# The order of the turned maxima, the sums and one normalised source in a transformer block

## The chip, the cores and the metric

The kernel runs on one core of a Trainium2 chip. The metric is the device time of one execution in microseconds (us), here the median of three runs. Beside it one further execution was profiled; all instruction times below come from that one.

## The reference

The block works on 16 sequences of 256 tokens with 256 features, all in float32, with 16 heads of 16 features:

```python
x_norm = modulate(_ln(x), shift_a, scale_a)
q, k, v = split(x_norm @ W_qkv + b_qkv)
x = x + gate_a * (softmax(q @ k.T / 4) @ v @ W_proj + b_proj)      # self-attention
q_c = _ln(x) @ W_qc + b_qc
k_c, v_c = split(_ln(context) @ W_kvc + b_kvc)
x = x + softmax(q_c @ k_c.T / 4) @ v_c @ W_cproj + b_cproj         # cross-attention
h = gelu(modulate(_ln(x), shift_m, scale_m) @ W_mlp1 + b_mlp1) @ W_mlp2 + b_mlp2
x = x + gate_m * h
```

shift, scale and gate come from `silu(cond) @ W_mod + b_mod`, one row per sequence. `_ln` subtracts a token's mean and divides by its standard deviation.

## The kernel before, in words

**Units and beats.** The 32 attentions (16 self, kind "s", and 16 cross, kind "c") are units, numbered 0 to 31: s0 to s4 first, then s and c in turn (unit 5 is s5, unit 6 is c0, and so on to unit 26, which is c10), then c11 to c15 as units 27 to 31. So an even unit between 6 and 26 is a cross-attention, an odd one from 5 to 25 a self-attention. After the units comes the MLP, which the change does not touch. A unit takes eight beats; `beat(n, k)` writes down all the work of beat k of unit n, for several units at once: unit n (`cur`) is being exponentiated and summed, unit n-1 (`prev`) is finishing, for unit n+1 (`nxt`) the row maxima are found, and the units n+2 to n+4 (`q2`, `q3`, `q4`) are being normalised, transposed and projected; `p1`, `p2`, `p3` are the output parts of the units n-1 to n-3. `lc`, `ls` and `lx` say of which kind such a unit is: `lx` is unit n+3 if that is a cross-attention (its source, the self-attention's result, is then normalised in this unit), `lc` is unit n+4 if cross, `ls` if self.

**Every engine runs its instructions in the order of the code.** A wrapper (`InOrder`, line 51, which is why the profile puts nearly all instructions on L51) keeps the program's order on TensorE, VectorE, ScalarE, GpSimd and the DMA queue of SyncE. So an instruction that waits holds up everything behind it on its engine.

**What a beat holds.** `visit` comes first: four matmuls into `s` (scores of unit n+1, from which VectorE takes row maxima into `mx`, a TENSOR_REDUCE), then four into `st` (scores of unit n in the other orientation). Then ScalarE turns `st` into exponentials `pt`. `s` and `st` have one buffer each: the next beat's `s` waits for this beat's reduce, its `st` for this beat's exponentials. In even beats `av_part` follows: 16 matmuls into `o` (values and, in a column of ones, sums). In odd beats a stretch of twelve pairs of projections (`lanes`) follows. In beats 0 and 2 two of the four transposes each of unit n+3's normalised source into `psT` (`turn`) stand behind `o`; where unit n+3 is a cross-attention, the four transposes of its other source (`psT_q`) stand behind `o` of beat 4.

**The maxima.** They must be subtracted before the exponential. That is done inside the matmul: row 63 of a half of `q` holds minus the maximum, row 63 of `k` holds ones. `m_part` does it twice per unit: it transposes `mx` (128x16) on TensorE into `psm`, negates it on ScalarE into `m`, and SyncE's DMA queue writes `m` into `q`. The second half of a unit's maxima is turned in its beat 0 (needed in its beat 4), the first half one beat 4 earlier, under the name `nxt` (needed in its beat 0).

**Banks.** `psm`, `psT` and `o` share two PSUM banks (tag "tr"); a tile gets the bank that came free first, and its first writer waits until the last reader of the tile before in that bank is done. `ps_k`, `ps_q`, `ps_v` and `ps_P` share two others in the same way (tag "gen"): in beat 5 `ps_k` gets the bank of `ps_q`, which VectorE reads last when it makes `l_q` (cross: `l_qc`) in beat 4.

**Sums and values.** When `o` of beat 2 or of beat 6 is copied to `oT` on ScalarE (`o_out`), `pull` fetches the sums `S` and the values `U` out of it by DMA; VectorE takes the reciprocal of `S` in beat 2 (in beat 3 where unit n+4 is a self-attention), `spread` and `back` bring it over DRAM into `R`, and GpSimd multiplies `U` by it in the next unit's beat 0 (`norm`, `high`, `low`), for the projection `ps_P` in beat 3.

**The last normalised source.** In beat 1, `lx.ln[1].steps` gets the statistics of unit n+3's self-attention result and normalises its two token tiles on GpSimd (`xn_q`, two TENSOR_SCALARs). For unit 31, that is in unit 28's time, the statistics are only taken in that beat.

Of the kernel before, what the change touches and what calls it, by code (L numbers as in the profile page):

```python
# [16 lines left out]
P = 128  # L17
# [4 lines left out]
def pixart_block(  # L22
# [273 lines left out]
    def layernorm(src, name):  # L296

        o = Box()

        def stats():  # L300
            o.st = work.tile([P, NT, 6], F32, tag="bnst", bufs=4, name=f"st_{name}")
            for t in range(NT):
                DVE.bn_stats(o.st[:, t], src()[:, t])

        def rstd(power=True):
            o.mv = work.tile([P, NT, 2], F32, tag="bnmv", bufs=4, name=f"mv_{name}")
            for t in range(NT):
                DVE.bn_aggr(o.mv[:, t], o.st[:, t])
            o.rs = work.tile([P, NT], F32, tag="rstd", bufs=4, name=f"rs_{name}")
            if power:  # L310
                o.pow()

        def pow():
            POOL.tensor_scalar(o.rs, o.mv[:, :, 1], EPS, None, ALU.add)
            POOL.tensor_tensor(o.rs, o.rs, mhalf, ALU.pow)

        def apply(eng=E_['LN'].get(name[0])):
            o.xn = work.tile([P, NT, H], F32, tag="xn", name=f"xn_{name}", bufs=3)
            if eng == "act":
                nb = work.tile([P, NT], F32, tag="rstd", name=f"nb_{name}", bufs=4)  # L320
                DVE.scalar_tensor_tensor(nb, o.mv[:, :, 0], -1.0, o.rs, ALU.mult, ALU.mult)
            for t in range(NT):
                if eng == "act":
                    ACT.activation(o.xn[:, t], src()[:, t], AF.Identity, bias=nb[:, t:t + 1],
                                   scale=o.rs[:, t:t + 1])
                else:
                    (DVE if eng == "dve" else POOL).tensor_scalar(
                        o.xn[:, t], src()[:, t], o.mv[:, t, 0:1], o.rs[:, t:t + 1],
                        ALU.subtract, ALU.mult)

        def stat(t):
            if t == 0:
                o.st = work.tile([P, NT, 6], F32, tag="bnst", bufs=4, name=f"st_{name}")
            DVE.bn_stats(o.st[:, t], src()[:, t])

        o.steps, o.pow, o.stat = [stats, rstd, apply], pow, stat
        return o
# [216 lines left out]
    def build_post(u):  # L554
# [15 lines left out]
            o.xg = work.tile([P, NT, H], F32, tag="xg", name=f"xg_{b}")  # L570
            POOL.tensor_tensor(o.xg, X[b], bc_t(G[b][:, 1]), ALU.add)

        def pull(G):

            if G == 0:
                o.U = work.tile([P, KC, N], F32, tag="U", name=f"U_{name}")
                o.S = work.tile([P, 32], F32, tag="S", name=f"S_{name}")
            SP.dma_start(o.S[64 * G:64 * G + 64], u.oT[1:98:32, G])
            SP.dma_start(o.U[64 * G:64 * G + 64], u.oT[0:P - 1:2, G])

        def recip():
            DVE.reciprocal(o.S, o.S)
# [82 lines left out]
                              AX.X, ALU.max)  # L665
        yield

    def m_part(u, hf):

        pst = ps_gen(f"psm_{u.n}_{hf}", SHORT)  # L670
        PE.transpose(pst[:16, :P], u.mx[:, hf].rearrange("p r a t -> p (r a t)"), ident)
        m = work.tile([16, P], F32R, tag="m", name=f"m_{u.n}_{hf}", bufs=1)
        ACT.mul(m, pst[:16, :P], -1.0)
        SP.dma_start(u.q[63:P:64, 4 * hf:4 * hf + 4, :].bitcast(F32), m.bitcast(F32))
# [19 lines left out]
    def exps():  # L694

        for f in later:
            f()
        later.clear()
# [275 lines left out]
        in_turn(*t)  # L974
        later.append(lambda: exp(units[n], k))

    def spare(n):
        p1, _, p3 = (v and v.post for v in map(unit, (n - 1, n - 2, n - 3)))
        if p3 and not p3.added:
            p3.add()  # L980
        if p1:
            p1.gate()

    def beat(n, k):
# [24 lines left out]
                p2.end()  # L1009
        visit(n, k)  # L1010
        if k == 0:
            if cur:
                m_part(cur, 1)
            exps()
            if q3 and q3.ready:
                q3.T[0].place()
            if prev:
                av_part(prev, 3)
            if q3 and q3.ready:
                q3.T[0].turn((0,))  # L1020
            if q2:
                q2.K.low()
                q2.K.send_low()
            if p2:
                p2.norm()
# [2 lines left out]
        elif k == 1:  # L1028
            exps()
            run(lanes(q2 and q2.Q, q2 and n and q2.V))  # L1030
            if prev:
                p1.pull(1)
            if lc:
                lc.ln[0].steps[0]()
            if lx:
                if lx.b in (0, B - 1):
                    lx.ln[1].steps[0]()
                lx.ln[1].steps[1]()
                lx.ln[1].steps[2]()
        elif k == 2:  # L1040
            exps()
            if cur:
# [10 lines left out]
        elif k == 3:  # L1053
# [14 lines left out]
            if prev and ls:  # L1068
                p1.recip()
                p1.spread()  # L1070
        elif k == 4:
            if nxt and lx:
                m_part(nxt, 0)
            exps()
            if nxt and not lx:
                m_part(nxt, 0)
            if alone:
                p2.end()
            if cur:
                av_part(cur, 1)  # L1080
            if lx:
                lx.T[1].turn()
            if q2:
# [1 line left out]
                q2.Q.send_low()  # L1085
            if q3 and q3.kind == "c":
                q3.T[0].rest_pool()
                spare(n)
            if ls:
                ls.ln[0].steps[1]()  # L1090
                ls.ln[0].steps[2]()
# [15 lines left out]
        elif k == 6:  # L1107
# [12 lines left out]
            if lx:  # L1120
                lx.T[1].full()
                lx.T[1].rest_pool()
        elif k == 7:
            exps()
            run(q3.vk if q3 and p2 else lanes(q3 and q3.V, q3 and q3.K))
# [110 lines left out]
```

## Time and profile before

| | |
|---|---|
| median of 3 runs | 748.76 us (744.28 to 749.36) |
| the profiled execution | 742.45 us, of which the program's span is 740.7 us |
| mean granted TensorE clock | 0.999 |
| busy in the span | TensorE 98%, its weight loads 81%, VectorE 77%, ScalarE 75%, GpSimd 71% |
| median instruction: transpose into psm | 277 ns, its weight load 87 ns, 64 of them |
| units 1 to 28 in the profile | about 15.8 us each where unit n+3 is a self-attention, 16.2 us where it is a cross-attention |

In the rows of the timeline stand: start in us from the span's start, duration in us, engine, line, operation, out<-in by the program's names, shapes, and how many instructions were merged into the row; in brackets the time for which the engine was idle before, and what ended it. PE is TensorE, PEld its weight loads, DVE VectorE, ACT ScalarE, POOL GpSimd, SPq the DMA queue of SyncE. The matmuls overlap, so what a matmul costs is read from the start of one to the start of the next, not from its duration.

### The profile page before, as it was taken

The numbers are of one execution on the slowest core, as the hardware profiler recorded it, in microseconds if no ns is written. First come the engines' busy times: TensorE is split into PE (matmuls) and PEld (weight loads), VectorE is DVE, ScalarE is ACT, GpSimd is POOL, SyncE is SP. The second block draws the span as 40 slices with busy tenths as digits, with TensorE's granted clock in tenths as the row PEclk, the third lists the DMA queues.
The fourth block names the chain that finished last, engine by engine and source line by source line (L and its number), as shares of the span: only waits on it lengthen the run. The fifth ranks groups of instructions, "written<-read, shape, count | busy, mean of one in ns | idle before, by whom it ended". The sixth has DMA issues, their size and how long they took to land.

```text
span 740.7 us, 22556 instructions
## 1 busy us (share of the span) xinstructions
PE 722.2 (98%) x9003; PEld 598.4 (81%) x9003; DVE 569.4 (77%) x882; ACT 556.1 (75%) x972; POOL 528.5 (71%) x525
## 2 busy tenths in 40 slices
PE   9999999999999999999999999999899999999997
PEld 8677777777777777777777787776479999999997
DVE  4778888878888887878788878778766877777762
ACT  5567888888888888887888888887766666666663
POOL 8465678797866868777686899985757676665663
PEclk9999999999999999999999999999999999999999
DMA  8365455544445455454555645545323132231311
GB/s 269 128 217 171 146 169 172 177 163 167 162 144 192 153 182 197 141 161 161 187 173 171 204 151 196 166 149 181 111 76 101 58 86 65 64 87 44 86 53 48
DMA packets 81388, 106.15 MB, mean 143 GB/s; under 512 B 16450, under 2 KB 44388, under 8 KB 81284
## 3 DMA queue, kind: packets, MB, share of 16 engines
q1 hardware_dynamic: 80180, 103.92, 43.3%
q8 instruction: 71, 1.16, 0.7%
q10 hardware_dynamic: 1104, 0.79, 0.4%
q14 instruction: 33, 0.27, 0.1%
HBM read 35.89 MB, written 8.98 MB: 61 GB/s over the span
## 4 chain that ended last, share of the span: by engine, by line
PE 92%; DVE 3%; ACT 2%; DMA 1%; issue 1%; POOL 1%; SPq 0%; ACTq 0%; POOLq 0%
PE s L51 18%; PE o L51 16%; PE st L51 14%; PE ph L51 13%; PE ps_P_s L51 4%; PE ps_k L51 3%; PE ps_v_s L51 3%; PE ps_kc L51 3%; PE ps_qc L51 3%; PE ps_v_c L51 2%; PE ps_q L51 2%; PE ps_P_c L51 2%; DVE mx L51 2%; PE psm L51 2%; PE psT_c L51 2%; PE psT_s L51 1%
## 5 line engine op out<-in xcount | busy, mean ns | idle before, releaser
L51 DVE TENSOR_REDUCE mx<-s 128x4 f32<-128x1024 f32 x252 | 307.7, 1221 | 89.2 <-PE s L51 88.7
L51 ACT ACTIVATE pt<-st 128x1024 f32<-128x1024 f32 x256 | 262.3, 1024 | 62.3 <-PE st L51 62.0
L51 PE MATMUL o<-pt,v 128*32 128x256 f32 x2048 | 137.1, 385 | 0.0
L51 PE MATMUL s<-big 63*128 63x256 f32 x1008 | 119.1, 307 | 5.5 <-DVE mx L51 4.0
L51 PE MATMUL st<-big 64*128 64x256 f32 (+1 forms) x1040 | 109.5, 284 | 3.1 <-ACT pt L51 1.7
L51 POOL TENSOR_TENSOR hl<-hf,hh 128x512 fp32r<-128x512 f32 x64 | 84.3, 1335 | 28.1 <-ACT hh L51 28.1
L51 PEld LDWEIGHTS s<-big 63*128 63x128 f32 x1008 | 79.0, 185 | 30.4 <-DVE mx L51 16.1
L51 PEld LDWEIGHTS st<-big 64*128 64x128 f32 (+1 forms) x1040 | 82.7, 186 | 6.6 <-ACT pt L51 3.4
L51 PEld LDWEIGHTS o<-pt,v 128*32 128x32 f32 x2048 | 53.4, 109 | 38.5
L51 ACT ACTIVATE hf<-ph,bT 128x256 f32<-128x256 f32 x120 | 50.4, 473 | 27.9 <-PE ph L51 27.9
L51 ACT ACTIVATE hh<-ph,bT 128x256 fp32r<-128x256 f32 x120 | 50.5, 472 | 20.9 <-PE st L51 9.8
L51 PE MATMUL ph<-wqch,wself 128*128 128x256 f32 x256 | 51.8, 286 | 1.3 <-ACT hh L51 1.3
L51 PE MATMUL ph<-wkch,wself 128*128 128x256 f32 x256 | 51.8, 286 | 0.0
L51 DVE TENSOR_SCALAR xn_m<-x,mv_m,rs_m 128x256 f32<-128x256 f32 x32 | 38.4, 1239 | 16.0 <-POOL rs_m L51 16.0
L51 PE MATMUL s<-big,hh 128*128 128x256 f32 x256 | 45.3, 276 | 0.0
L51 PE MATMUL st<-big,hh 128*128 128x256 f32 x256 | 45.0, 276 | 0.0
L51 PEld LDWEIGHTS ph<-wqch,wself 128*128 128x128 f32 x256 | 41.9, 191 | 1.9 <-ACT hh L51 1.5
L51 PEld LDWEIGHTS ph<-wkch,wself 128*128 128x128 f32 x256 | 41.9, 191 | 0.3
L51 POOL TENSOR_SCALAR xn_q<-x,mv_q,rs_q 128x256 f32<-128x256 f32 x32 | 38.9, 1225 | 1.7
L51 POOL TENSOR_SCALAR xn_c<-c,mv_c,rs_c 128x256 f32<-128x256 f32 x32 | 38.9, 1225 | 1.7
L51 PEld LDWEIGHTS s<-big,hh 128*128 128x128 f32 x256 | 38.8, 188 | 0.0
L51 PEld LDWEIGHTS st<-big,hh 128*128 128x128 f32 x256 | 38.8, 188 | 0.0
(214 smaller groups left out, 2215.7 us busy)
## 6 DMA issues: line engine op xcount, KB each, us to landing
big<-h_kc SPq DMA_DIRECT2D x32, 256.0 KB
big<-h_qc SPq DMA_DIRECT2D x32, 256.0 KB
big<-h_k SPq DMA_DIRECT2D x31, 256.0 KB
big<-h_q SPq DMA_DIRECT2D x31, 256.0 KB
big<-l_k SPq DMA_DIRECT2D x16, 256.0 KB
big<-l_q SPq DMA_DIRECT2D x16, 256.0 KB
g<-gd SPq DMA_DIRECT2D x16, 256.0 KB
U_s<-oT SPq DMA_DIRECT2D x32, 128.0 KB
```

Source lines behind the costliest of these rows:

```text
L51: i = f(*a, **k)
```

## The change

**Beat 0.** The transpose of the unit's second half of maxima moves from ahead of `o` to behind it, and no longer has a tile of its own: it writes into the upper half of the `psT` tile that the two transposes of unit n+3's source, right behind it, fill from below (in units 1 to 28; later there is no `psT`, and the maxima keep their own tile). ScalarE's negation moves from ahead of the exponentials to behind the copy `oT`. The pull of the sums moves from beat 1 to beat 0, ahead of the DMA of `l_k` (`send_low`); the pull of the values stays.

**Beat 4.** Where unit n+3 is a self-attention (units 0, 1, 2 and the even ones to 22), the transpose of the next unit's first half of maxima moves from ahead of `o` to behind it.

**Unit 28.** Only the first token tile of unit 31's source is normalised on GpSimd; the second is normalised on ScalarE in beat 4, between the negated maxima and the exponentials, with a bias that VectorE works out in beat 3. **Units 24 and 26.** The sum `xg` on GpSimd (`gate`) moves from beat 4 to beat 6.

```diff
+        def apply_half(t):
+            if t == 0:
+                o.xn = work.tile([P, NT, H], F32, tag="xn", name=f"xn_{name}", bufs=3)
+                POOL.tensor_scalar(o.xn[:, t], src()[:, t], o.mv[:, t, 0:1], o.rs[:, t:t + 1],
+                                   ALU.subtract, ALU.mult)
+            else:
+                ACT.activation(o.xn[:, t], src()[:, t], AF.Identity, bias=o.nb[:, t:t + 1],
+                               scale=o.rs[:, t:t + 1])
+        def apply_bias():
+            o.nb = work.tile([P, NT], F32, tag="rstd", name=f"nb_{name}", bufs=4)
+            DVE.scalar_tensor_tensor(o.nb, o.mv[:, :, 0], -1.0, o.rs, ALU.mult, ALU.mult)
...
-    def m_part(u, hf):
+    def m_part(u, hf, pst=None):
+        m_row(u, hf, m_turn(u, hf, pst))
-        pst = ps_gen(f"psm_{u.n}_{hf}", SHORT)
+    def m_turn(u, hf, pst=None):
+        if pst is None:
+            pst = ps_gen(f"psm_{u.n}_{hf}", SHORT)
         PE.transpose(pst[:16, :P], u.mx[:, hf].rearrange("p r a t -> p (r a t)"), ident)
+        return pst
+    def m_row(u, hf, pst):
         m = work.tile([16, P], F32R, tag="m", name=f"m_{u.n}_{hf}", bufs=1)
         ACT.mul(m, pst[:16, :P], -1.0)
         SP.dma_start(u.q[63:P:64, 4 * hf:4 * hf + 4, :].bitcast(F32), m.bitcast(F32))
...
         if k == 0:
-            if cur:
-                m_part(cur, 1)
             exps()
-            if q3 and q3.ready:
-                q3.T[0].place()
             if prev:
                 av_part(prev, 3)
             if q3 and q3.ready:
+                q3.T[0].place()
+                pst = m_turn(cur, 1, q3.T[0].ps[:, N:])
                 q3.T[0].turn((0,))
+            else:
+                pst = m_turn(cur, 1)
+            m_row(cur, 1, pst)
             if q2:
                 q2.K.low()
+            if prev:
+                p1.pull_sums(1)
+            if q2:
                 q2.K.send_low()
...
         elif k == 1:
...
             if prev:
-                p1.pull(1)
+                p1.pull_values(1)
...
-                lx.ln[1].steps[2]()
+                if lx.b == B - 1:
+                    lx.ln[1].apply_half(0)
+                else:
+                    lx.ln[1].steps[2]()
...
+            if lx and lx.b == B - 1:
+                lx.ln[1].apply_bias()
         elif k == 4:
             if nxt and lx:
                 m_part(nxt, 0)
+            if lx and lx.b == B - 1:
+                lx.ln[1].apply_half(1)
             exps()
-            if nxt and not lx:
-                m_part(nxt, 0)
             if alone:
                 p2.end()
             if cur:
                 av_part(cur, 1)
+            if nxt and not lx:
+                m_part(nxt, 0)
...
-                spare(n)
+                spare(n, not lc)
...
         elif k == 6:
...
                 lx.T[1].rest_pool()
+                if lc:
+                    p1.gate()
```

The added `apply_bias` call stands at the end of beat 3.

Beat 0 of unit 17 on TensorE and on the DMA queue. The rows name an operation, what it writes and reads, and a shape; `mx` are the maxima, `xn_c` the normalised source of unit 20, `o_2` the values of unit 16, `st` and `s` the scores. Before, the beat's first rows, up to the first matmuls into `o`, and then its last ones, from the last matmuls into `o` to the next beat's `s` and `st`:

```order
L51 MATMUL s<-big_75 128x256 x4
L51 MATMUL st<-big_77 128x256 x4
L51 MATMUL psm_1_5791<-ident,mx_5478 16x128
L51 MATMUL o_2_5722<-pt_6_5720,v_79 32x256
```

```order
L51 MATMUL o_2_5722<-pt_6_5720,v_79 32x256
L51 MATMUL o_2_5722<-pt_7_5747,v_79 32x256
L51 MATMUL psT_c_5798<-ident,xn_c_5704 128x128 x2
L51 MATMUL s<-big_75 128x256 x4
L51 MATMUL st<-big_77 128x256 x4
```

With the change, the end of the same beat:

```order
L51 MATMUL o_2_5706<-pt_6_5704,v_79 32x256
L51 MATMUL o_2_5706<-pt_7_5731,v_79 32x256
L51 MATMUL psT_c_5786<-ident,mx_5463 16x128
L51 MATMUL psT_c_5786<-ident,xn_c_5688 128x128 x2
L51 MATMUL s<-big_75 128x256 x4
L51 MATMUL st<-big_77 128x256 x4
```

The maxima's transpose has moved from between `st` and `o` to between `o` and `psT`, into the tile of `psT`. On the DMA queue the same beat and the next read, before and with the change (`m_1` the maxima, `l_kc` a part of unit 20's keys; here at unit 18):

```order
L51 DMA big_76<-h_kc_6726 32x4x512 x2
L51 DMA big_77<-m_1_6743 2x8x128
L51 DMA big_76<-l_kc_6760 32x4x512
L51 DMA S_s_6683<-oT_6649 64x1x32
L51 DMA U_s_6682<-oT_6649 64x512
```

```order
L51 DMA big_76<-h_kc_6707 32x4x512 x2
L51 DMA big_77<-m_1_6737 2x8x128
L51 DMA S_s_6664<-oT_6630 64x1x32
L51 DMA big_76<-l_kc_6740 32x4x512
L51 DMA U_s_6663<-oT_6630 64x512
```

The sums have passed one DMA. Beat 4 of unit 22 on TensorE, an even unit (`o_0` its own values, `mx` the maxima of unit 23, `ps_k` the keys of unit 25 in beat 5), before and then with the change from the last inputs of `o` on:

```order
L51 MATMUL st<-big_76 128x256 x4
L51 MATMUL psm_0_7527<-ident,mx_7362 16x128
L51 MATMUL o_0_7450<-pt_2_7448,v_79 32x256
L51 MATMUL o_0_7450<-pt_3_7482,v_79 32x256
```

```order
L51 MATMUL o_0_7428<-pt_2_7426,v_79 32x256
L51 MATMUL o_0_7428<-pt_3_7460,v_79 32x256
L51 MATMUL psm_0_7513<-ident,mx_7341 16x128
L51 MATMUL s<-big_77 128x256 x4
L51 MATMUL st<-big_76 128x256 x4
L51 MATMUL ps_k_7533<-xTh_s_7456,wself 128x256
```

The transpose now stands between `o` and the next beat's `s`. Beat 4 of unit 28 on ScalarE with the change (`h_qc` the queries of unit 30, `m_0` the maxima of unit 29, `x_15` the self-attention result of the last sequence, `pt_4` the exponentials); before, the fourth row was not there:

```order
L51 ACTIVATE pt_3_9396<-st 128x1024
L51 ACTIVATE h_qc_9425<-ps_qc_9319,bP 128x256 x2
L51 ACTIVATE m_0_9441<-psm_0_9439 16x128
L51 ACTIVATE xn_q_9354<-x_15_9263,nb_q_9423,rs_q_9351 128x256
L51 ACTIVATE pt_4_9445<-st 128x1024
L51 ACTIVATE pt_5_9474<-st 128x1024
```

Half of the normalisation has come in ahead of the exponentials.

More of the change, by code (lines that the diff above doesn't have):

```diff
@@ L578, in pull, with pull_values @@
             SP.dma_start(o.S[64 * G:64 * G + 64], u.oT[1:98:32, G])
+        def pull_values(G):
             SP.dma_start(o.U[64 * G:64 * G + 64], u.oT[0:P - 1:2, G])
+        def pull(G):
+            pull_sums(G)
+            pull_values(G)
+        o.pull_sums, o.pull_values = pull_sums, pull_values
         def recip():
@@ L975, in visit, with spare @@
         later.append(lambda: exp(units[n], k))
-    def spare(n):
+    def spare(n, gate=True):
         p1, _, p3 = (v and v.post for v in map(unit, (n - 1, n - 2, n - 3)))
@@ L980, in spare @@
             p3.add()
-        if p1:
+        if p1 and gate:
             p1.gate()
```

3 lines of the change are left out of this document (2 added, 1 removed).

## The prediction

> **What bounds the kernel now.** I read the page first: which engine is busy, and which carries the chain that ended last.
>
> ```profile
> PE 722.2 (98%) x9003; PEld 598.4 (81%) x9003; DVE 569.4 (77%) x882; ACT 556.1 (75%) x972; POOL 528.5 (71%) x525
> PE 92%; DVE 3%; ACT 2%; DMA 1%; issue 1%; POOL 1%; SPq 0%; ACTq 0%; POOLq 0%
> ```
>
> TensorE is busy for 98% of the span and makes 92% of the chain. Nothing that another engine saves counts by itself; what counts is TensorE's pace from one group of matmuls to the next, and the few places where it waits. So I read the timeline of TensorE, start to start. Unit 17, beat 0 and the head of beat 1, then the end of beat 4:
>
> ```profile
> 307.16 0.48 PE L51 MATMUL s<-big 63*128 63x256 f32 x4
> 307.48 0.41 PE L51 MATMUL st<-big 64*128 64x256 f32 x4
> 307.81 0.28 PE L51 MATMUL psm<-ident,mx 128*16 128x128 f32 x1
> 308.02 1.07 PE L51 MATMUL o<-pt,v 128*32 128x256 f32 x16
> 309.02 0.44 PE L51 MATMUL psT_c<-ident,xn_c 128*128 128x128 f32 x2
> 309.39 0.50 PE L51 MATMUL s<-big 63*128 63x256 f32 x4
> 309.73 0.40 PE L51 MATMUL st<-big 64*128 64x256 f32 x4
> ...
> 317.18 0.66 PE L51 MATMUL psT_q<-ident,xn_q 128*128 128x128 f32 x4
> 317.77 0.50 PE L51 MATMUL s<-big 63*128 63x256 f32 x4
> ```
>
> No row has an idle bracket: TensorE goes from group to group at its own pace. From `st` to what follows it takes 0.33, `psm` costs 0.21 (307.81 to 308.02), `o` 1.00, two transposes 0.37 (309.02 to 309.39), four of them 0.59 (317.18 to 317.77).
>
> **Beat 0, TensorE: the main term.** The transpose of the maxima leaves its place ahead of `o`, which saves the 0.21, and becomes a third transpose in the `psT` group. Two more transposes there cost 0.59 - 0.37 = 0.22, one costs 0.11. Net -0.10 a unit. The merged form stands in units 1 to 28, so 28 x 0.10 = 2.8 us. The trace does not show a 16-column transpose ahead of a 128-column one, so bounds: the pair of transposes lasts 0.44, of which the second is 0.27 to 0.28 (the `psm` row), so that its first step takes up to 0.17; a merged turn at 0.17 saves only 0.04 a unit (1.1 us). On the other side stands the weight load:
>
> ```profile
> L51 PEld LDWEIGHTS psm<-ident,mx x64: 86/87/88, 28.9 to 532.3; 128*16 128x16 f32 x64
> L51 PEld LDWEIGHTS psT_c<-ident,xn_c x64: 137/140/143, 85.4 to 490.1; 128*128 128x128 f32 x64
> ```
>
> In these rows (shortest, median, longest in ns) loading the maxima takes 87 ns against 140 ns, so the turn may cost 0.05 less than its neighbours, 0.06 instead of 0.11: -0.15 a unit, 4.2 us. I take 0.11, the step that two added transposes show. The Trainium skill (TensorE: Matmul & The Clock Gate, section "LDWEIGHTS (loading the stationary operand)") gives a load the time of its columns over 1.2 a ns, which for 16 columns would be an estimated 13 ns and would put the term near 28 x 0.20 = 5.6 us; the measured 87 ns speaks against it, and the sum goes by the rows.
>
> Is the tenth kept? In beat 1 `s` waits for the reduce of beat 0 and `ps_q` for `l_k`; both follow beat 0's `s` on VectorE. What ScalarE does I read in unit 16, beat 0 and the head of beat 1, with the two DMA issues that move:
>
> ```profile
> 292.30 0.27 ACT L51 ACTIVATE m<-psm 16x128 fp32r<-16x128 f32 x1
> 292.48 1.00 ACT L51 ACTIVATE pt<-st 128x1024 f32<-128x1024 f32 x1
> 293.38 0.56 ACT L51 COPY oT<-o 128x512 f32<-128x512 f32 x1
> 294.36 1.03 ACT L51 ACTIVATE pt<-st 128x1024 f32<-128x1024 f32 x1 [0.42 <-PE st L51]
> 293.68 0.58 SPq L51 DMA_DIRECT2D big<-m  x1
> 295.00 0.60 SPq L51 DMA_DIRECT2D S_s<-oT  x1
> ```
>
> ScalarE stands idle for 0.42 before the exponentials of beat 1, so it has room for the negated maxima behind `oT`. The exponentials of beat 0 start 0.18 sooner (292.30 instead of 292.48). So the tenth is kept. Behind the moved negation stand those exponentials of beat 1 and their `st`; its new wait is for the `psT` group, which ends before `oT` does.
>
> **The sums.** `m` now follows `oT`, which ends at about 293.76 when the exponentials start 0.18 sooner; its DMA goes from 293.68 to about 294.0, and the sums behind it from 295.00 to about 294.65: 0.35 earlier. `l_k` goes out some 0.9 later, near 295.3, and is first read by unit 17's first `s` at 307.16, 11 us on, so I cost that at nothing, and the values likewise. Does the earlier sum help? In an even unit the reciprocal stands on VectorE ahead of beat 3's reduce. In the profile it was clearly late once, in unit 18:
>
> ```profile
> 327.18 0.60 SPq L51 DMA_DIRECT2D S_s<-oT  x1
> 329.48 0.51 PE L51 MATMUL s<-big 63*128 63x256 f32 x4
> 330.45 0.35 DVE L51 RECIPROCAL S_s<-S_s 128x32 f32<-128x32 f32 x1 [1.23 <-DMA S_s<-oT]
> 330.72 1.16 DVE L51 TENSOR_REDUCE mx<-s 128x4 f32<-128x1024 f32 x1
> 331.94 0.51 PE L51 MATMUL s<-big 63*128 63x256 f32 x4 [0.30 <-DVE mx L51]
> ```
>
> The reduce was held back and `s` of beat 4 with it: 2.46 after `s` of beat 3 (329.48 to 331.94), where the two reduces of unit 22 (below) start 1.93 apart: 0.53 lost. Bounds 0 (another execution may not have it) and 0.53; I take 0.4, near the 0.35 that the sums gain.
>
> **Unit 28.** Here the source is what comes last:
>
> ```profile
> 492.62 2.43 POOL L51 TENSOR_SCALAR xn_q<-x,mv_q,rs_q 128x256 f32<-128x256 f32 x2
> 493.18 1.07 PE L51 MATMUL o<-pt,v 128*32 128x256 f32 x16
> 495.11 0.55 PE L51 MATMUL psT_q<-ident,xn_q 128*128 128x128 f32 x3 [0.60 <-POOL xn_q L51]
> 495.58 0.50 PE L51 MATMUL s<-big 63*128 63x256 f32 x4
> 493.33 0.27 ACT L51 ACTIVATE m<-psm 16x128 fp32r<-16x128 f32 x1
> 493.51 1.00 ACT L51 ACTIVATE pt<-st 128x1024 f32<-128x1024 f32 x1
> ```
>
> `o` starts at 493.18; without a wait the next `s` would come 1.00 + 0.59 later, at 494.77, and it came at 495.58: 0.81 lost. With the change GpSimd's half is done at about 493.85 (half of 2.43), ScalarE's stands behind `m` (free at 493.51); for 128x256 elements I bound it by the rows of unit 16 from both sides, 0.27 for the 16x128 of `m` and 0.56 for the 128x512 of `oT`: done by 493.8 to 494.07, before `o` ends at 494.18. The whole 0.81 goes. The exponentials behind it slip to 494.07 at most and end at 495.07; the `st` that waits for them would stand at 494.77 + 0.34 = 495.11 (0.34 as from 309.39 to 309.73), so it is just covered, and what ScalarE's half takes beyond 0.56 would cost as much. I take 0.8, bounds 0.4 (a cover gone by 0.4) and 0.81. The bias on VectorE is one short instruction ahead of a reduce that TensorE does not wait for in that beat; the later `xg` in units 24 and 26 stands on GpSimd behind transfers with two beats to spare: nothing.
>
> **Beat 4 of the even units: nothing.** Unit 22, TensorE and VectorE:
>
> ```profile
> 396.16 0.44 PE L51 MATMUL st<-big 64*128 64x256 f32 x4
> 396.68 0.27 PE L51 MATMUL psm<-ident,mx 128*16 128x128 f32 x1
> 396.88 1.07 PE L51 MATMUL o<-pt,v 128*32 128x256 f32 x16
> 397.88 0.50 PE L51 MATMUL s<-big 63*128 63x256 f32 x4
> 398.22 0.40 PE L51 MATMUL st<-big 64*128 64x256 f32 x4
> 398.50 0.38 PE L51 MATMUL ps_k<-xTh_s,wself 64*128 64x256 f32 x1
> ...
> 394.52 1.22 DVE L51 TENSOR_REDUCE mx<-s 128x4 f32<-128x1024 f32 x1 [0.56 <-PE s L51]
> 395.67 0.86 DVE L51 SCALAR_TENSOR_TENSOR xTl_s<-psT_s,sc,xTh_s 128x256 fp32r<-128x256 f32 x2
> 396.45 1.22 DVE L51 TENSOR_REDUCE mx<-s 128x4 f32<-128x1024 f32 x1
> 397.58 0.87 DVE L51 SCALAR_TENSOR_TENSOR l_qc<-ps_qc,bP,h_qc 128x256 fp32r<-128x256 f32 x2
> ```
>
> `psm` follows `st` by 0.52 instead of 0.33: it waits 0.19 for its bank, that of `psT_s`, which VectorE reads until 396.53. Moved behind `o`, the transpose no longer waits, and the next `s` would come at 396.16 + 0.33 + 1.00 + 0.26 = 397.75 (0.26 is 0.37 less one step of 0.11) instead of 397.88: -0.13. But the next gate stands two rows on: `ps_k` needs the bank that `l_qc` reads until 397.58 + 0.87 = 398.45, and starts at 398.50. VectorE's four rows follow one another without a gap from beat 3's reduce on, so that gate does not move. The wait changes its place, 0 us. Bounds -0.13 and +0.06 (`psm` without a wait cost 0.21, now 0.26) for 13 units: -1.7 to +0.8.
>
> **Sum.** 2.8 + 0.8 + 0.4 = 4.0 us off the profiled execution, 742.45 to 738.45. The median of the runs shown is 748.76, 6.3 above that execution (the lowest run is 744.28), so I put the forecast at 748.76 - 4.0 = 744.8; that is 0.5% faster, and under 1% a measurement of this kernel can hardly tell from no change.
>
> **The rivals.** (B) *The tenth does not come, or unit 28's exponentials become late.* The merged turn costs 0.17 to 0.21 because the group's start-up is paid by whatever comes first. Then 28 x 0.02 + 0.8 + 0.4 = about 1.8: 747.0. For it: the 0.17 first step. Against it: the second transpose then pays 0.11 instead of 0.17, which gives the sum above. (C) *Beat 4 pays as well,* if `ps_k` is not held by `l_qc`: 4.0 + 13 x 0.13 = 5.7: 743.1. For it: 0.19 of wait goes in 13 units. Against it: 398.45 and 398.50. The Trainium skill (TensorEngine Tiling (Array Packing), section "Key Properties") says that a change of the tiling mode drains the engine; by that rule beat 0 loses one of its changes of shape, in agreement with 0.21 against 0.11, and beat 4 keeps its number, which speaks against C too. (D) *Slower: ScalarE becomes the bound in beat 0.* The negation now waits for `psT` and stands ahead of beat 1's exponentials. Price and point: if it comes so late (a late source of unit n+3 holds `psT`) that the 0.42 of idle time less the tenth, and some 0.3 until the next `st`, are used up, each further 0.1 costs 2.8 us over 28 units; 0.4 more costs 11, less the 4.0: 756. Against it: `psT`'s source is ready when `o` ends in the rows above. (E) *The change doesn't do what it says for the sums*: they stay behind a slow `m`; that is 0.4 less, inside the range.
>
> **How the numbers follow.** Forecast 0.60, B 0.18, C 0.14, D 0.08. The bounds of the unknown costs give 1.1 + 0.4 + 0 - 0.8 = 0.7 to 4.2 + 0.8 + 0.5 + 1.7 = 7.2 off, 748.1 to 741.6 by the median; the runs shown lie up to 4.5 below their median and 0.6 above, so I let the range reach from 739.0 to 749.5, without D. Faster by over 1% (under 741.3) needs C and a low level of the runs: 0.13. Slower by over 1% (over 756.2) is about half of D and other mishaps: 0.06. Within 1%: 0.81.
>
> **What would show it.** In the profile after: 36 transposes into `psm` instead of 64; from `st` to `st` over beat 0 2.15 instead of 2.25 in units 1 to 28; in beat 4 of unit 28 no wait for `xn_q` and 2.55 instead of 3.37; in even units `psm` behind `o`, `s` up to 0.13 sooner and `ps_k` as late as before; the reciprocal without a wait of over 1 us. I am wrong if the step from the maxima to the first transpose of `psT` is over 0.2, if the exponentials of beat 1 start over 0.3 later against their `st`, or if the even units get shorter by over 0.2.

## The result and the profile after

| | before | after |
|---|---|---|
| median of 20 runs each | 743.32 us (741.95 to 749.36) | 739.76 us (737.80 to 745.67) |
| ratio after to before, 95% interval | | 0.9959 (0.9944 to 0.9974) |
| profiled execution, its span | 742.45, 740.7 us | 741.72, 739.9 us |

The change takes 0.4% off, 3.0 us of 743.3 (1.9 to 4.2); the forecast was 4.0 us. The three runs of before from which the forecast's 744.8 us was counted lay above the level of the twenty; in every other run of that kernel above 747 us whose clock is on record, the mean granted clock was 0.991 or less. The two profiled executions differ by only 0.7 us, so the trace has to be read by stages, not by its span.

The page of the changed kernel, the busy times and the shares of the chain that ended last:

```profile
PE 723.2 (98%) x9003; PEld 601.6 (81%) x9003; DVE 569.9 (77%) x883; ACT 557.5 (75%) x973; POOL 526.8 (71%) x524
PE 91%; DVE 4%; ACT 1%; DMA 1%; POOL 1%; issue 1%; SPq 1%; ACTq 0%; POOLq 0%
```

TensorE is as full as before; VectorE has one point more of the chain. So the pace is read again from start to start. TensorE and VectorE in the changed kernel's timeline, unit 17, beat 0 and the head of beat 1 (PEld are weight loads):

```profile
308.03 0.41 PE L51 MATMUL st<-big 64*128 64x256 f32 x4
308.36 1.07 PE L51 MATMUL o<-pt,v 128*32 128x256 f32 x16
309.37 0.28 PE L51 MATMUL psT_c<-ident,mx 128*16 128x128 f32 x1
309.38 0.87 DVE L51 SCALAR_TENSOR_TENSOR l_k<-ps_k,bqkv,h_k 128x256 fp32r<-128x256 f32 x2
309.48 0.38 PE L51 MATMUL psT_c<-ident,xn_c 128*128 128x128 f32 x2
309.79 0.51 PE L51 MATMUL s<-big 63*128 63x256 f32 x4
310.13 0.40 PE L51 MATMUL st<-big 64*128 64x256 f32 x4
310.30 0.18 PEld L51 LDWEIGHTS ps_q<-xTh_s,wself 64*128 64x128 f32 x1
310.37 0.31 PE L51 MATMUL ps_q<-xTh_s,wself 64*128 64x256 f32 x1
```

The 0.21 between `st` and `o` is gone: `o` follows `st` by 0.33. The group of three transposes takes 309.37 to 309.79, 0.42, where the pair took 0.37. So the turned maxima cost 0.05 instead of 0.21, and beat 0 lasts 2.10 instead of 2.25. Then look at the last two rows: `l_k` ends at 309.38 + 0.87 = 310.25, and only then does the weight load of `ps_q` start. In the same beat of the kernel before,

```profile
308.83 0.87 DVE L51 SCALAR_TENSOR_TENSOR l_k<-ps_k,bqkv,h_k 128x256 fp32r<-128x256 f32 x2
309.86 0.30 PEld L51 LDWEIGHTS ps_q<-xTh_s,wself 64*128 64x128 f32 x2
```

`l_k` had been done, at 309.70, for 0.16 when TensorE came to it.

What the stages took, from `st` to `st` (unit 0 and unit 31 stand for start and tail):

| us | before | after | forecast |
|---|---|---|---|
| beat 0, median of units 4 to 27 | 2.25 | 2.10 | 2.15 |
| beats 1 and 2 together, the same units | 3.93 | 3.97 | 3.93 |
| beats 4 and 5, mean of units 4, 6 ... 22 | 4.06 | 4.06 | 4.06 |
| beat 3 of unit 18 | 2.45 | 1.84 | some 2.0 |
| beat 4 of unit 28 | 3.36 | 2.55 | 2.55 |
| units 1 to 28 | 449.26 | 444.83 | 445.3 |
| unit 0 | 17.28 | 19.46 | 17.28 |
| unit 31, beats 0 to 6 | 14.96 | 16.76 | 14.96 |

In units 1 to 28 the change did what was forecast and a little more, 4.4 us. At both ends it lost 4.0 of them in this execution, and neither end was in the sum. The experiments ask which of that belongs to the change.

Unit 31 first. TensorE, SyncE's queue and the chain that normalises the first source of the MLP (`x` loaded, added to on GpSimd, normalised into `xn_m`, transposed into `psT_m`), before:

```profile
531.91 0.50 PE L51 MATMUL st<-big 64*128 64x256 f32 x4 [1.18 <-ACT pt L51]
533.00 0.57 SPq L51 DMA_DIRECT2D big<-m  x1
533.62 0.40 SPq L51 DMA_DIRECT2D x<-x2d  x1
537.53 1.28 POOL L51 TENSOR_TENSOR x<-x,cb 128x512 f32<-128x512 f32 x1 [1.30 <-DMA x<-x2d]
541.38 0.74 DVE L51 TENSOR_SCALAR xn_m<-x,mv_m,rs_m 128x256 f32<-128x256 f32 x2 [1.21 <-POOL rs_m L51]
542.55 0.66 PE L51 MATMUL psT_m<-ident,xn_m 128*128 128x128 f32 x4
```

and with the change:

```profile
529.73 0.50 PE L51 MATMUL st<-big 64*128 64x256 f32 x4 [1.18 <-ACT pt L51]
531.17 0.28 PE L51 MATMUL psm<-ident,mx 128*16 128x128 f32 x1
531.94 0.66 PE L51 MATMUL psT_m<-ident,xn_m 128*128 128x128 f32 x4 [0.50 <-ACT oT L51]
532.07 0.58 SPq L51 DMA_DIRECT2D big<-m  x1
532.70 0.56 SPq L51 DMA_DIRECT2D S_c<-oT  x1
533.30 0.46 SPq L51 DMA_DIRECT2D x<-x2d  x1
536.86 1.30 POOL L51 TENSOR_TENSOR x<-x,cb 128x512 f32<-128x512 f32 x1 [2.54 <-DMA x<-x2d]
541.95 0.87 PE L51 MATMUL psT_m<-ident,xn_m 128*128 128x128 f32 x4 [1.13 <-DVE xn_m L51]
```

Two new waits. The load `x<-x2d` goes out 3.57 after the unit's first `st` (529.73 to 533.30) instead of 1.71 (531.91 to 533.62): SyncE's queue now has the later `m` and the sums ahead of it, and both wait for TensorE or ScalarE. TensorE waits 1.13 for `xn_m` at the end of that chain; beat 4 takes 3.43 instead of 2.02. And psT_m waits 0.50 for `oT`. In unit 31 the maxima keep a tile of their own, and turning them behind `o` changes the rotation of the two banks: the maxima take the free one, and psT_m, which follows in this unit alone, gets that of `o`.

### The profile page after: what moved, and what is told of

It is laid out like the page before. It is cut to its first block, busy times and chain, and to the rows that moved or that the text cites. A ratio compares the mean times of both kernels' runs of the same rounds, so it can differ in the third digit from the quotient of the medians.

```text
span 739.9 us, 22479 instructions
## 1 busy us (share of the span) xinstructions
PE 723.2 (98%) x9003; PEld 601.6 (81%) x9003; DVE 569.9 (77%) x883; ACT 557.5 (75%) x973; POOL 526.8 (71%) x524
## 4 chain that ended last, share of the span: by engine, by line
PE 91%; DVE 4%; ACT 1%; DMA 1%; POOL 1%; issue 1%; SPq 1%; ACTq 0%; POOLq 0%
PE s L51 18%; PE o L51 15%; PE st L51 14%; PE ph L51 12%; PE ps_k L51 4%; PE ps_qc L51 4%; PE ps_P_s L51 3%; PE ps_q L51 3%; PE ps_v_s L51 3%; PE ps_kc L51 3%; PE ps_v_c L51 3%; DVE mx L51 2%; PE ps_P_c L51 2%; PE psT_c L51 2%; PE psT_s L51 1%; PE psT_q L51 1%
```

## The experiments

All ratios are to runs of the kernel before on the same chip. The kernels 9 to 11 leave out a part of the result and serve only to find a wait.

| kernel | median us | ratio, 95% interval |
|---|---|---|
| 1 changed, units 0 and 29 to 31 as before | 738.80 | 0.9938 (0.9915 to 0.9962) |
| the same, again | 738.43 | 0.9938 (0.9906 to 0.9971) |
| 2 changed, again | 739.87 | 0.9967 (0.9941 to 0.9993) |
| 3 before, again | 743.56 | 1.0007 (0.9974 to 1.0039) |
| 4 merged turn alone | 740.36 | 0.9962 (0.9942 to 0.9982) |
| 5 changed, maxima in a bank of their own | 764.05 | 1.0278 (1.0241 to 1.0316) |
| 6 beat 4 alone | 742.79 | 0.9986 (0.9958 to 1.0015) |
| 7 unit 28's half alone | 743.41 | 0.9998 (0.9979 to 1.0017) |
| 8 earlier sums alone | 742.81 | 1.0006 (0.9990 to 1.0022) |
| 9 changed, without 13 low halves of queries | 737.33 | 0.9921 (0.9900 to 0.9942) |
| 10 before, without the same 13 | 742.15 | 0.9979 (0.9961 to 0.9996) |
| 11 changed, without the low halves `l_k` | 740.15 | 0.9945 (0.9916 to 0.9974) |

**1. The tail.**

```diff
         if k == 0:
+            merged = q3 and q3.ready
+            if cur and not merged:
+                m_part(cur, 1)
             exps()
...
-            if q3 and q3.ready:
+            if merged:
...
-            else:
-                pst = m_turn(cur, 1)
-            m_row(cur, 1, pst)
+                m_row(cur, 1, pst)
...
-            if prev:
+            if prev and merged:
                 p1.pull_sums(1)
...
             if prev:
+                if not (q3 and n):
+                    p1.pull_sums(1)
                 p1.pull_values(1)
```

> The changed kernel, except that in the units without a `psT` (0, 29, 30 and 31) beat 0 is as before: the maxima are turned ahead of `o`, negated ahead of the exponentials, and the sums are pulled in beat 1 behind the DMAs of `m` and of the load of x. Theory: unit 31 gave back about 1.8 us with the change, 0.4 because the maxima now share the bank that `oT` is copied from (a wait of 0.50 for ScalarE in the trace), and 1.4 because the load x<-x2d stands later in SyncE's queue and everything up to the normalised source of the MLP waits for it. Then this kernel is 1.8 us faster than the changed kernel, some 5 us faster than the kernel before (ratio 0.993), x<-x2d is issued 1.7 us after the first `st` of unit 31 instead of 3.6, and beat 4 of unit 31 lasts about 2.0 us instead of 3.43. Rival: the tail of that one profile was chance; then the time is that of the changed kernel (ratio 0.996) and beat 4 of unit 31 is long or short without regard to the order.

> The changed kernel with beat 0 as before in the units 0, 29, 30 and 31, once more, since its interval and that of the changed kernel still overlap. Theory: ratio to the kernel before 0.993 to 0.994, unit 31 again 14.8 us. Rival: the gain over the changed kernel was chance, 0.996.

Measured: 0.9938 both times, about 4.6 us faster than before, and faster than the changed kernel, whose two medians of 739.76 and 739.87 stand against 738.80 and 738.43 here. The intervals still overlap, so the times alone don't show the difference; the trace shows where it lies. The same rows as above in the first of these profiles:

```profile
526.78 0.50 PE L51 MATMUL st<-big 64*128 64x256 f32 x4 [1.18 <-ACT pt L51]
528.42 0.66 PE L51 MATMUL psT_m<-ident,xn_m 128*128 128x128 f32 x4
528.50 0.39 SPq L51 DMA_DIRECT2D x<-x2d  x1
532.19 1.36 POOL L51 TENSOR_TENSOR x<-x,cb 128x512 f32<-128x512 f32 x1 [0.79 <-DMA x<-x2d]
537.29 0.66 PE L51 MATMUL psT_m<-ident,xn_m 128*128 128x128 f32 x4
```

The load goes out 1.72 after `st`, neither psT_m waits, beat 4 lasts 2.02 and unit 31 14.82 (16.76 with the change). In the second profile the load went out at the same place but took 4.2 us instead of 3.7 until GpSimd had it, and unit 31 came to 15.68: in these profiles the order moves this end by about 1.8 us, a slow DMA by up to 0.9 us. Over all fourteen profiles the load goes out 3.56 to 3.58 after `st` in the five with the change's order in unit 31, and 1.71 to 2.04 in the eight with the old one; experiment 8, with the sums alone moved, stands between them (3.07). By its medians this kernel is the fastest of those that compute everything.

**2 and 3. Both kernels again.**

> The changed kernel once more, for a second profile and for its time beside the others. Theory: units 1 to 28 take 444.8 us as in the first profile (449.3 before), beat 4 of unit 31 is again 3.4 us, and unit 0, which took 19.5 us in the first profile against 17.3 before, comes out near 17.3, because the change does nothing in unit 0 but set the order of transposes that wait for the first loads. Rival: unit 0 is again near 19.5; then the change costs 2 us at the start.

> The kernel before once more, for a second profile. Theory: units 1 to 28 again 449.3 us, unit 18's beat 3 again longer than unit 22's by some 0.5 us because the reciprocal waits for its sums, unit 0 between 17 and 20 us. Rival for the sums: unit 18's beat 3 is 1.9 us here, so that its late reciprocal was chance and the earlier sums are worth nothing.

Unit 31 of the changed kernel was again 16.61, with 3.30 in beat 4: the tail belongs to the change. Unit 0 was 16.76 instead of 19.46, so that the start doesn't. What it was is told in the last section. Units 1 to 28 took 445.62 (after) and 448.98 (before). In the kernel before, unit 18 was on time now, and other units were late, here unit 16, whose reciprocal starts only at 298.12 and made beat 3 2.12 long (the profile puts its wait down to the load of the values, which was issued right behind that of the sums):

```profile
298.12 0.35 DVE L51 RECIPROCAL S_s<-S_s 128x32 f32<-128x32 f32 x1 [0.91 <-DMA U_s<-oT]
```

So the place was chance; that it happens somewhere was not (8, below).

**4. The merged turn alone.** The kernel before with the change's `m_turn`, `m_row` and beat 0 in units 1 to 28:

```diff
         if k == 0:
-            if cur:
+            merged = q3 and q3.ready
+            if cur and not merged:
                 m_part(cur, 1)
             exps()
-            if q3 and q3.ready:
-                q3.T[0].place()
             if prev:
                 av_part(prev, 3)
-            if q3 and q3.ready:
+            if merged:
+                q3.T[0].place()
+                pst = m_turn(cur, 1, q3.T[0].ps[:, N:])
                 q3.T[0].turn((0,))
+                m_row(cur, 1, pst)
```

> The kernel before, with one part of the change alone: in units 1 to 28 the maxima of beat 0 are turned in one group and one bank with `psT`, and negated behind `oT`; the sums, beat 4 and unit 28 are as before, and units 0 and 29 to 31 too. Theory from the two traces: beat 0 is 0.15 us shorter and beat 1 gives 0.03 back, 28 x 0.12 = 3.4 us off the time before (ratio 0.9955). The forecast's term was 28 x 0.10 = 2.8 (0.9962). Rival: the group's start-up is paid by whichever transpose comes first; 28 x 0.02 = 0.6 (0.999).

Measured 0.9962, 2.8 us, with an interval of 1.3 to 4.3 that holds the 3.4 expected here as well as the forecast's 2.8. Beat 0 is 2.10, beats 1 and 2 together 3.96, so 0.11 a unit and 28 x 0.11 = 3.1 by the trace. In this profile units 1 to 28 as a whole took only 2.3 less (446.98): the sums, still in their old place, were late by 0.4 more than in the first profile of before, and beat 7 of unit 6 was 0.3 longer. The rival's 0.999 is outside of the interval.

**5. The bank.**

```diff
             if q3 and q3.ready:
+                m_part(cur, 1)
                 q3.T[0].place()
-                pst = m_turn(cur, 1, q3.T[0].ps[:, N:])
                 q3.T[0].turn((0,))
             else:
-                pst = m_turn(cur, 1)
-            m_row(cur, 1, pst)
+                m_part(cur, 1)
```

> The changed kernel, except that in units 1 to 28 the maxima of beat 0, turned behind `o` as in the change, keep a tile of their own instead of the upper half of `psT`. Theory: what pays is that the maxima stand in one group with `psT`, and the shared bank is what makes that possible: with a tile of its own the maxima take the bank that is free, `psT` then gets the bank of `o` and waits until ScalarE has copied it to `oT`, as psT_m did in unit 31 with 0.50. So beat 0 gets 0.5 longer in each unit, some 10 to 14 us slower than the changed kernel (ratio to the kernel before 1.010 to 1.015). Rival: only the place counts; then the time is that of the changed kernel (0.996).

Measured 1.0278, 24 us slower than the changed kernel instead of 10 to 14; the mechanism holds, its price was 0.86 a unit instead of 0.5 (beat 0 is 2.96). Unit 17 of this kernel, TensorE with its weight load and ScalarE:

```profile
320.46 0.28 PE L51 MATMUL psm<-ident,mx 128*16 128x128 f32 x1
320.64 0.60 ACT L51 COPY oT<-o 128x512 f32<-128x512 f32 x1
321.10 0.26 ACT L51 ACTIVATE m<-psm 16x128 fp32r<-16x128 f32 x1
321.35 0.20 PEld L51 LDWEIGHTS psT_c<-ident,xn_c 128*128 128x128 f32 x2 [0.81 <-POOL xTh_as L51]
321.38 0.41 PE L51 MATMUL psT_c<-ident,xn_c 128*128 128x128 f32 x2 [0.64 <-ACT m L51]
```

The trace names `m` (to 321.36) and a cast on GpSimd as the releasers because they ended last. But the weight load of the transposes starts at 321.35, before `m` has ended, and in all 28 units it starts 0.11 after the end of `oT` (here 321.24), for which the transposes wait in the program. So it is the bank of `o`: the same order of the same instructions takes 3 us off or puts some 20 on by the bank alone.

**6. Beat 4 alone.**

```diff
             exps()
-            if nxt and not lx:
-                m_part(nxt, 0)
             if alone:
                 p2.end()
             if cur:
                 av_part(cur, 1)
+            if nxt and not lx:
+                m_part(nxt, 0)
```

> The kernel before, with only the move in beat 4 of the units 0, 1, 2 and the even ones to 22: the maxima turned behind `o`. Theory (the forecast's term): the wait moves on to `ps_k`, beats 4 and 5 together stay at 4.06 (2.06 and 2.01 become about 1.89 and 2.15), 0 to -0.3 us (ratio 1.000). Rival C: `ps_k` is not held; beats 4 and 5 come to 3.93, 13 x 0.13 = 1.7 us faster (0.9977).

Measured 0.9986 with 1 inside; beat 4 1.92 instead of 2.06, beat 5 2.14 instead of 2.01, together 4.06. The wait changed its place, as forecast. In the changed kernel the rows of unit 22 are:

```profile
396.75 0.28 PE L51 MATMUL psm<-ident,mx 128*16 128x128 f32 x1
396.79 0.87 DVE L51 SCALAR_TENSOR_TENSOR l_qc<-ps_qc,bP,h_qc 128x256 fp32r<-128x256 f32 x2
396.95 0.51 PE L51 MATMUL s<-big 63*128 63x256 f32 x4
397.30 0.40 PE L51 MATMUL st<-big 64*128 64x256 f32 x4
397.71 0.18 PEld L51 LDWEIGHTS ps_k<-xTh_s,wself 64*128 64x128 f32 x1 [0.22 <-DVE l_qc L51]
```

`psm` to `s` is 0.20 and without a wait; `l_qc` ends at 397.66 and the weight load of `ps_k` starts at 397.71.

**9 and 10. The gate behind beat 4.** The same edit in both kernels:

```diff
             if q2:
-                q2.Q.low()
+                if nxt and not lx and q3:
+                    q2.Q.no_low()
+                else:
+                    q2.Q.low()
                 q2.Q.send_low()
```

where `no_low` is a memset of the tile to zero on GpSimd.

> The changed kernel, except that in 13 units (0, 1, 2 and the even ones from 4 to 22) VectorE doesn't compute the low halves `l_qc` of the queries: GpSimd sets them to zero, so that part of the sum is left out. Theory: `l_qc` is the gate of `ps_k` in beat 5. Without it the moved maxima do pay: beats 4 and 5 of the even units come to about 3.75 instead of 4.04, 13 x 0.29 = 3.8 us faster than the changed kernel. Rival: `ps_k` waits for something else; 4.04 stays and the time too.

> The kernel before, except that in the same 13 units the low halves of the queries are set to zero by GpSimd instead of being computed on VectorE, which leaves out the same part. Theory: beats 4 and 5 of the even units come to about 3.91 instead of 4.06, 13 x 0.15 = 2 us faster than the kernel before; the wait for the bank of `psT_s` in front of the maxima (0.19) stays, and against the changed kernel without these halves 13 x 0.13 = 1.7 us are missing. Rival: the maxima's wait for their bank doesn't matter; both come to the same sum of the two beats.

Beats 4 and 5 of the even units came to 3.78 in the changed kernel and 3.92 in the kernel before, where 3.75 and 3.91 were expected and 4.06 stood in both. With the gate gone the move pays its 0.13, the number that the forecast had worked out for rival C. The ratios agree: 0.9979 is -1.6 us (expected -2), and 0.9921 lies 2.8 to 3.4 us below the changed kernel's 0.9959 and 0.9967 (expected 3.8). In the kernel of experiment 9, `ps_k` of unit 22 follows at its own pace:

```profile
392.95 0.28 PE L51 MATMUL psm<-ident,mx 128*16 128x128 f32 x1
393.16 0.50 PE L51 MATMUL s<-big 63*128 63x256 f32 x4
393.50 0.40 PE L51 MATMUL st<-big 64*128 64x256 f32 x4
393.74 0.28 PE L51 MATMUL ps_k<-xTh_s,wself 64*128 64x256 f32 x1
```

`st` to `ps_k` is 0.24, against 0.41 (397.30 to 397.71) with the gate.

**7. Unit 28 alone.** The kernel before with the change's `apply_half` and `apply_bias`, and without the later `xg`:

```diff
         elif k == 1:
...
-                lx.ln[1].steps[2]()
+                if lx.b == B - 1:
+                    lx.ln[1].apply_half(0)
+                else:
+                    lx.ln[1].steps[2]()
...
+            if lx and lx.b == B - 1:
+                lx.ln[1].apply_bias()
         elif k == 4:
             if nxt and lx:
                 m_part(nxt, 0)
+            if lx and lx.b == B - 1:
+                lx.ln[1].apply_half(1)
             exps()
```

> The kernel before, with only unit 28's change: half of the last source normalised on ScalarE. Theory: beat 4 of unit 28 lasts 2.55 instead of 3.36, 0.8 us off, and nothing else moves (ratio 0.9989). Rival: what beat 4 gains is given back in unit 28's or 29's next beats because ScalarE's exponentials are later; then 0.

Beat 4 of unit 28 lasted 2.55, and its beats 5 to 7 and unit 29 changed by less than 0.1 (5.59 against 5.53, and 15.33 against 15.37). The ratio 0.9998 can't tell 0.1% from nothing; the trace can.

**8. The sums alone.** (`pull` is cut into `pull_sums` and `pull_values`; that part of the edit is left out here.)

```diff
             if q2:
                 q2.K.low()
+            if prev:
+                p1.pull_sums(1)
+            if q2:
                 q2.K.send_low()
...
             if prev:
-                p1.pull(1)
+                p1.pull_values(1)
```

> The kernel before, with only the sums pulled ahead of the DMA of `l_k`, in beat 0. Theory: in each of the three profiles with the sums in beat 1 some reciprocals came late and held back a reduce (the beats lost 0.6; 0.3, 0.1 and 0.5; 0.3, 0.7 and 0.1), in none of the three with the sums in beat 0; so here no beat 3 is longer than 2.0, and 0.6 to 1.0 us go; in unit 31 the load x<-x2d stands one DMA (0.6 us) later, of which the 0.4 that the normalised source had to spare are free: 0.2 back. Ratio 0.9992. Rival: late reciprocals go on at other places, since a slow DMA of the sums is not a matter of the place in the queue; ratio 1.000.

Half a miss. No beat 3 of units 1 to 28 was over 1.9, as expected. By how much beat 3 of single units was longer than usual (some 1.88, in unit 30 2.26) sums to 0.6, 1.0, 1.0, 0.6, 1.3 and 1.5 us in the six profiles with the sums in beat 1, and in the eight with the sums in beat 0 to nothing five times, and 0.5, 0.5 and 0.3. That is 0.8 us on average. Units 1 to 28 as a whole took only 0.3 less than in the first profile of before (448.96), since beat 7 of unit 20 was 0.4 longer. And unit 31 gave back 1.0, not 0.2. In its queue:

```profile
532.54 0.57 SPq L51 DMA_DIRECT2D big<-m  x1
533.91 0.56 SPq L51 DMA_DIRECT2D S_c<-oT  x1
534.52 0.45 SPq L51 DMA_DIRECT2D x<-x2d  x1
```

The sums don't only take their 0.6 of the queue. They wait in it until `oT` is done (533.88 by the trace), from 533.11 to 533.91, and `x<-x2d` stands behind them: it goes out 3.07 after the unit's `st` (531.45 here) instead of 1.71. Gain and loss about cancel, and the ratio can't tell the rest from 1.

**11. What ends beat 1 now.**

```diff
             if q2:
-                q2.K.low()
+                if q3 and q3.ready and prev:
+                    q2.K.no_low()
+                else:
+                    q2.K.low()
```

> The changed kernel, except that in units 1 to 28 VectorE doesn't compute the low halves `l_k` of the keys in beat 0; GpSimd sets them to zero, so that part of the sum is left out. In both kernels `l_k` ends 2.22 us after the beat's `st`; before, the first weight load of `ps_q` came at 2.38, now at 2.27, so that with the change `l_k` has become the gate of beat 1. Theory: that gate is why beat 1 lasts 1.91 instead of 1.86 with the change; without it beat 1 is back at 1.86 with beat 0 at 2.10, 28 x 0.05 = 1.4 us faster than the changed kernel (ratio to before 0.994). Rival: beat 1 is longer for another reason, say the negation on ScalarE in front of its exponentials; then beat 1 stays at 1.91.

Beat 1 alone did not come back to 1.86 as expected: it is 1.85 in some units and 1.90 in others, and where it is 1.90 beat 2 is 0.04 shorter. The kernel before has a few such units too, so the two are to be read together: 3.93 here, as in the kernel before, against 3.97 with the change. The weight load of `ps_q` shows the gate directly. By the median of units 4 to 27 it follows beat 1's `st` by some 0.12 before, 0.17 with the change, and 0.12 again without `l_k`. The rival, the negation on ScalarE, stands behind `oT` in this kernel too, so it is not what takes the 0.04. The time, 740.15 us, doesn't show the 1.0 us: units 25 and 27 lost 0.9 (0.35 and 0.6 in their beats 4; GpSimd has the memsets on top there, and whether they are the cause was not followed), and the profiled execution had stretches at half clock at both ends (last section). The gate is shown, its worth in the time isn't.

## Why the prediction was right, and where not

**Bound.** TensorE's pace from group to group carried the argument, and every gain was found in it.

**Beat 0: right in the sum, by two errors that cancel.** Forecast -0.10 a unit and nothing in beat 1. The turn costs 0.05, not 0.11: the bound that was read from the weight loads (87 ns against 140) was the better value, not the step that an added 128-column transpose takes. The step from the maxima to the first transpose is 0.11 (309.37 to 309.48), and from there to the second it is 0.11 too (0.38 less the 0.27 of the last one), where the pair had paid 0.17 at its head. The group's first step has become shorter by 0.06, about what the two loads differ by. In the changed kernel's rows (shortest, median, longest in ns) the load of the maxima keeps its time:

```profile
L51 PEld LDWEIGHTS psT_c<-ident,mx x16: 86/88/88, 87.3 to 484.6; 128*16 128x16 f32 x16
L51 PEld LDWEIGHTS psT_c<-ident,xn_c x64: 137/141/145, 87.3 to 488.7; 128*128 128x128 f32 x64
```

No run isolates the load as the cause of the 0.05. By the rule of the Trainium skill (TensorE: Matmul & The Clock Gate, section "LDWEIGHTS (loading the stationary operand)") the term would, as an estimate, have been some 5.6 us; 88 ns and 3.1 us speak against it. The prediction's remark that beat 0 loses one of its changes of shape is not borne out by the rows: before, the shapes from `st` to the next `s` are `64*128`, `128*16`, `128*32`, `128*128`, `63*128`, and with the change `64*128`, `128*32`, `128*16`, `128*128`, `63*128`, four changes each. The second error is the sentence that the tenth is kept. It named `l_k`, but put a number only on ScalarE, which had the room. But `l_k` on VectorE ends 2.22 after the beat's `st` in both kernels (307.48 to 309.70, 308.03 to 310.25), and with beat 0 at 2.10 that has become later than TensorE's own pace. 0.04 a unit goes there (11). Net 28 x 0.11 = 3.1 instead of 2.8.

**Sums: right in kind, 0.8 instead of 0.4 by the beats 3.** A late reciprocal is not one event in unit 18 but one to six in each execution, at changing places.

**Unit 28: right,** 0.81. ScalarE's half, whose duration was bounded by 0.27 and 0.56, is

```profile
492.15 0.58 ACT L51 ACTIVATE xn_q<-x,nb_q,rs_q 128x256 f32<-128x256 f32 x1
492.82 0.44 PE L51 MATMUL psT_q<-ident,xn_q 128*128 128x128 f32 x2
```

just over the upper bound, and still under `o` (491.82 to 492.82), which covers it.

**Beat 4 of the even units: right,** to the gate and to the 0.13 that stands behind it (9, 10). The later `xg` in units 24 and 26 left no trace (the units took 16.11 and 16.13 before and 16.03 twice after, and beat 0 with beats 1 and 2 accounts for the 0.1).

**The tail: missed, -1.8 us of the gain.** Two steps failed. "I cost that at nothing" weighed what the moved `m` and sums delay by one DMA, `l_k` in units 1 to 28. In unit 31 it is the load x<-x2d that is behind them, and on it hangs the source of the MLP. And the units without a `psT` were left out of the sum, although there the maxima move too and take another bank. Neither D nor E covered it.

**The sum.** Beat 0, the sums, unit 28, some 0.1 in beat 4 of the even units and the tail give -3.1 - 0.8 - 0.8 - 0.1 + 1.8 = -3.0. The ratio gives 3.0 with an interval of 1.9 to 4.2, and the stretches at half clock and the late beats 7 of the last section are in no term, so that the agreement to a tenth is chance. That the forecast's 4.0 came near is luck in part: its terms were worth 4.8, and what it left out took 1.8. The 739.76 us lie below 741.6, the low end that its bounds gave; only the room that it left for the level of the runs reaches them. B (the tenth doesn't come) falls with the 2.10, C with the 4.06, D with the exponentials of beat 1, which start 0.45 after their `st` (before: 0.44) and still wait for it:

```profile
310.58 1.03 ACT L51 ACTIVATE pt<-st 128x1024 f32<-128x1024 f32 x1 [0.27 <-PE st L51]
```

## What to carry to other kernels

An instruction that is moved on an in-order queue moves its wait along, and all that stands behind it in *every* iteration: ask the question for the first and last ones too, where other neighbours stand. Before counting a saving, look for the gate that comes next on another engine and say how far it is behind (here 0.16 for `l_k` in beat 0, nothing for `l_qc` in beat 4). Where tiles share banks in rotation, one more tile between two others is a question of who gets whose bank: the same order cost 0.7 a unit or saved 0.1.

## What was not expected of the hardware

The granted TensorE clock fell to one half for short stretches in five places within the units of the fourteen profiles: in unit 0 of the first changed kernel and of experiment 11, in unit 31 of experiments 4, 7 and 11. Windows of the changed kernel and then of experiment 4; the third column from the right is the granted clock:

```profile
36.50:37.50 1.00, 0.80 (x6) 0.68 (x8) 0.85 (x3) 0.15 (x2) 0.00 (x0) 0.99 0.84 280
37.50:44.00 6.50, 6.50 (x46) 5.01 (x47) 3.11 (x4) 2.05 (x2) 1.88 (x2) 0.50 0.53 181
44.00:44.50 0.50, 0.50 (x4) 0.37 (x2) 0.00 (x0) 0.00 (x0) 0.00 (x0) 0.68 0.47 82
```

```profile
530.50:534.00 3.50, 3.50 (x26) 1.68 (x19) 1.98 (x5) 2.46 (x5) 2.93 (x4) 0.51 0.28 87
534.00:536.00 2.00, 2.00 (x24) 0.87 (x22) 1.97 (x2) 1.34 (x2) 1.84 (x3) 1.00 0.18 66
```

From the shares at their edges the stretches last 6.8 us twice (unit 0) and 3.4 us three times (unit 31). The first made unit 0 19.46 instead of 17.2 us, 2.2 of the 4.0 that the changed kernel seemed to lose at its ends; the one in experiment 4 made unit 31 16.09. The Trainium skill (TensorE: Matmul & The Clock Gate, section "What's actually happening") says that the clock is either full or half, judged by free-running windows of 3413 ns in which the array was busy or idle. The lengths, one and two such windows, agree. What decides that a window counts as idle is not shown: all five stand in or next to stretches in which TensorE waits (1.18 at the head of unit 31, the first loads in unit 0), but the same waits went without a drop in the other profiles. Whether the change, which puts the maxima behind `o` in unit 0 too, makes the drop there likelier (two of five profiles with that order, none of nine without) stays open. The mean granted clock on record for each run says a little more, though not where a drop fell: it was 0.994 or less in 9 of 50 runs with that order and in 14 of 172 without. So drops come with either order, and these counts don't settle whether the change makes them likelier.

A wait of `s` at the end of unit 6 stays open too. Its beat 7 lasted 2.15 to 2.55 instead of 1.83 in four of the fourteen profiles (experiments 2, 4 and 9 and the second profile of experiment 1), and beat 7 of one other unit was 0.3 to 0.7 too long in experiments 8, 9 and 11. None of the five profiles with beat 0 and the sums as before has such a beat, six of the nine others do. So this may be a cost of the change that no term covers; no run shows its cause.
